# Block 3 of a four-block transformer kernel: the weighted values of a turn in one piece behind the next turn's scores

## The chip, the core and the metric

The kernel runs on one core of a Trainium2 chip. A core has five engines that run side by side, each through its own instructions in its own order: TensorE (PE: matmuls; its weight loads are shown apart as PEld), VectorE (DVE), ScalarE (ACT), GpSimd (POOL) and SyncE (SP), which issues DMAs. They wait for each other through semaphores. Matmul results land in PSUM, which is small (here eight banks of 128 x 512 f32), and another engine copies them to SBUF. The metric is the device time of one execution in microseconds (us); the number given for a kernel is the median of its runs.

## The reference, cut to what matters

Four blocks follow each other on x of shape (2, 1024, 128): an attention with an MLP (two layers), a windowed attention with an MLP (two layers), a local attention with a pooled "latent" part, and a routed mixture of experts. The change is in the third:

```python
def _L1_attn_ref(x, ...):                     # 16 heads of 8, window 128
    qkv = x @ qkv_w + qkv_b
    q, k, v = jnp.split(qkv, 3, axis=-1)
    local = _local_attention(heads(q), heads(k), heads(v))
    pooled = x.reshape(B, nlat, chunk, D).mean(axis=2)
    ...
    remote = lat_out @ rout_w + rout_b
    gate = jax.nn.sigmoid(local @ gl_w + remote_h @ gr_w)
    mixed = gate * local + (1.0 - gate) * remote_h
    return mixed @ out_w + out_b

def _local_attention(q, k, v):
    ...
    scores = jnp.einsum('bhnqd,bhnkd->bhnqk', qb, kb) * scale
    scores = jnp.where(allowed, scores, NEG)
    attn = jax.nn.softmax(scores, axis=-1)
    out = jnp.einsum('bhnqk,bhnkd->bhnqd', attn, vb)
```

Each query sees at most 128 keys before it, so a tile of 128 queries needs the keys of its own tile and of the one before.

## The kernel before, in words

All four blocks stand in one program. In each block the order of the instructions on TensorE, VectorE, ScalarE and GpSimd is written out by hand: they are issued in the order in which the Python code calls them, and each engine runs its own in that order.

Block 3 is the class BlockC (from L1025; stage_c at L1019 runs it). It goes through 16 query tiles (b, m), two sequences of eight, and does each in two **turns** (ip 0 and 1); a turn holds eight heads as two slots of four. Its `both()` issues one turn, as a software pipeline of three turns: the scores of this turn, the transposes of the weights of the turn before (`self.turns`), and the weighted values of the turn before that (`self.values`).

- `score()` (L1241) gives four steps. The first issues on TensorE the masks (L1258, 4 bf16 matmuls that write the mask into PSUM) and the scores (L1262, 32-row matmuls), and on VectorE two row maxima (L1267), one for each of the two score tiles s0 and s1. The second is four exponentials of the first tile on ScalarE (L1271) and, unless a sort is under way, the subtraction for the second tile on VectorE (L1278). The third, in a sort, is four more exponentials (L1271). The fourth, without one, is one wide exponential (L1288).
- `turn()` (L1292), a **group of transposes**: four 128 x 128 transposes of the weights (L1299) into one of two PSUM buffers named tr, and ScalarE's copy of them to pT (L1300). A turn has four such groups.
- `value()` (L1302), a **group of values**: four matmuls whose weights are 32 columns wide (L1310), each in another quarter of the array's columns; in f32 they are 8 loads and 8 passes in the trace. They add up in a bank named o, which `k.mm()` hands out from a pool of two.
- `finish()` (L1316), once a tile: ScalarE copies o to oT (L1319); one beat later or more, `rest()` transposes it (L1326), divides by the sums on VectorE (L1329, L1332) and calls `done()`, which starts `gate()` (L1420) when a group of tiles is complete. From there come the products on GpSimd (L1435), the output matmul (L1472) and the first steps of block 4 (`Front.tiles`, L1541, with L1554, L1560 and the sort of the router's scores, L1524 and L1525).

What else there is to do comes from the pipe (`Pipe`, L109): a list of steps by **beat**. `both()` has four beats; at the head of each, `beat()` issues the steps that are due then, ahead of that beat's own work. `later(0, f)` puts f at the head of the next beat to come. Steps that need a bank of the pool of two take one beat each, in beats 1 to 7 of every eight; the foreign steps that the prediction speaks of (projections L1158 and L1165; the latent part L1358, L1359, L1374, L1380, L1397, L1403; L1326; L1472) stand there. `front.todo` holds the passes of the sort on VectorE; one is issued at the end of each beat.

So in the kernel before a beat of a full turn holds: due steps; one step of this turn's scores; one group of transposes; one group of values; one pass of the sort. The values and finish() of the last turns follow when the scores are through (`while self.turns or self.values or pipe.due`), and behind them block 4 fills TensorE with expert matmuls (L1665) while the sort and the routing run on VectorE.

Of the kernel before, what the change touches and what calls it, by code (L numbers as in the profile page):

```python
# [539 lines left out]
class BlockB:  # L540
# [175 lines left out]
    def project(self, l, b, m, later):  # L716
# [78 lines left out]
        for at, rank, f in (  # L795
            (0, 0, queries), (1, 1, values), (1, 2, square), (6 if first else 2, 1, keep), (2, 2, sums),
            (3, 0, root), (4, 0, scale), (5, 1, cross), (6, 1, straight), (7, 1, both),
        ):
            if not first or f not in early:
                later(at, f, rank=rank)  # L800
# [224 lines left out]
class BlockC:  # L1025
# [61 lines left out]
    def both(self, b=None, m=None, ip=None, nxt=None):  # L1087

        now = self.score(b, m, ip) if m is not None else []
        for i in range(4):  # L1090
            self.pipe.beat()
            for f in now[i : i + 1] + self.turns[i : i + 1] + self.values[i : i + 1]:
                f()
            if nxt and i == 0:
                self.mask(*nxt)
            if not self.hold:
                for f in self.front.todo[:1]:
                    f()
                del self.front.todo[:1]
        for f in self.values[4:]:  # L1100
            self.pipe.later(0, f)
        self.values = self.turns[4:]
        self.turns = []
        if m is not None:
            nk = 1 if m == 0 else 2
            pairs = [(half, t) for half in range(2) for t in range(nk)]
            none = [lambda: None] * (4 - len(pairs))
            self.turns = [lambda p=p: self.turn(b, m, 2 * p[0] + ip, p[1]) for p in pairs] + none
            if nk == 1:
                self.turns = self.turns[:1] + self.turns[2:3] + self.turns[1:2] + self.turns[3:]  # L1110
            self.turns += [lambda p=p: self.value(b, m, 2 * p[0] + ip, p[1]) for p in pairs] + none
            if ip == 1:
                self.turns.append(lambda: self.finish(b, m))
# [703 lines left out]
def route(k, p1, front, fill):  # L1817
# [84 lines left out]
    for step in (8, 4, 2, 1, 0):  # L1902
# [70 lines left out]
    both = junk[:, :P]  # L1973
    nc.vector.scalar_tensor_tensor(
        both, ps[:, :P], 1.0, k.mat["pair"], ALU.mult, ALU.mult, accum_out=v
    )
    nc.vector.tensor_tensor(v, v, none, ALU.add)
# [268 lines left out]
```

## Time and profile before

| | us |
|---|---|
| three runs | 1286.54, 1290.57, 1290.62 |
| median of the runs | 1290.57 |
| span of the profiled execution, first to last instruction | 1288.7 |
| block 1 | about 0 to 366 |
| block 2 | about 366 to 757 |
| block 3 | about 757 to 1046 |
| sort and routing of block 4, with expert matmuls beside them | about 1046 to 1146 |
| rest of block 4 | about 1146 to 1289 |
| first and last masks of block 3 (L1258) | 766.75 and 1027.23 |

The profile is of one execution; the trace holds no other time of it than its span, so sums are made against 1288.7. Over the span TensorE is busy 90%, VectorE 68%, ScalarE 50% and GpSimd 38%.

How its lines read: a group line gives source line, engine, operation, out<-in by the program's names, shapes and count; then busy us and the mean ns of one; then the engine's idle time just ahead of these instructions and what ended it. A row in order of time gives the start (us from the span's start), how long the row lasts, engine, line and what it is; in brackets the idle time ahead of it. Rows of equal instructions are merged (x4, x8). A line of busy time by stretch gives the stretch, its length, then PE, PEld, DVE, ACT and POOL busy us with counts, the clock granted to TensorE (1.00 is full), DMA share and GB/s.

### The profile page before, as it was taken

The numbers are of one execution on the slowest core, as the hardware profiler recorded it, in microseconds if no ns is written. First come the engines' busy times: TensorE is split into PE (matmuls) and PEld (weight loads), VectorE is DVE, ScalarE is ACT, GpSimd is POOL, SyncE is SP. The second block draws the span as 40 slices with busy tenths as digits, with TensorE's granted clock in tenths as the row PEclk, the third lists the DMA queues.
The fourth block names the chain that finished last, engine by engine and source line by source line (L and its number), as shares of the span: only waits on it lengthen the run. The fifth ranks groups of instructions, "written<-read, shape, count | busy, mean of one in ns | idle before, by whom it ended". The sixth has DMA issues, their size and how long they took to land.

```text
span 1288.7 us, 23486 instructions
## 1 busy us (share of the span) xinstructions
PE 1158.7 (90%) x9441; PEld 747.7 (58%) x9441; DVE 870.0 (68%) x1782; ACT 646.3 (50%) x1216; POOL 488.6 (38%) x565
## 2 busy tenths in 40 slices
PE   5999999999688999999999877989999978997798
PEld 3656766666356656666656634546555543433688
DVE  5556666555587776776777435556677979999763
ACT  5445455444355665665664545656665755441000
POOL 1523333232588776676686442221222211100000
PEclk9899999999899999999999988989998989999799
DMA  9000000000010000010100021000000000000000
GB/s 297 2 1 1 1 1 1 2 1 1 18 26 22 22 22 18 22 26 18 26 22 18 5 78 41 1 1 1 2 1 1 2 1 1 0 17 1 25 17 17
DMA packets 19840, 25.18 MB, mean 20 GB/s; under 512 B 2762, under 2 KB 13716, under 8 KB 19476
## 3 DMA queue, kind: packets, MB, share of 16 engines
q1 hardware_dynamic: 19076, 23.02, 6.4%
q8 instruction: 75, 1.23, 0.4%
q10 hardware_dynamic: 656, 0.66, 0.2%
q14 instruction: 33, 0.27, 0.1%
HBM read 13.32 MB, written 1.05 MB: 11 GB/s over the span
## 4 chain that ended last, share of the span: by engine, by line
PE 61%; DVE 23%; ACT 7%; POOL 5%; issue 4%; DMA 0%; DVEq 0%; POOLq 0%; ACTq 0%
PE big L1665 6%; PE mm L1748 5%; PE bank L407 4%; PE s L372 4%; PE bank L960 4%; PE s L727 3%; PE s L835 3%; PE bank L880 2%; PE s L1262 2%; PE s L1258 2%; PE bank L467 2%; PE tr L1299 2%; DVE nm L1267 2%; PE bank L488 2%; DVE nm L378 2%
## 5 line engine op out<-in xcount | busy, mean ns | idle before, releaser
L1267 DVE TENSOR_REDUCE nm<-s 128x4 f32<-128x1024 f32 (+1 forms) x64 | 71.0, 1152 | 60.1 <-PE s L1262 59.8
L378 DVE TENSOR_REDUCE nm<-s 128x1 f32<-128x1024 f32 x64 | 75.1, 1216 | 51.4 <-PE s L372 51.4
L1300 ACT COPY pT<-tr 128x512 f32<-128x512 f32 x120 | 70.0, 598 | 73.2 <-PE tr L1299 73.0
L774 POOL TENSOR_TENSOR t<-raw,tab 128x512 f32<-128x512 f32 x62 | 77.1, 1266 | 75.0 <-DVE raw L765 75.0
L1299 PE MATMUL tr<-ident,pr 128*128 128x128 f32 x480 | 77.2, 284 | 2.6 <-ACT pT L1300 2.3
L736 ACT ACTIVATE sq<-s 128x1024 f32<-128x1024 f32 x32 | 32.7, 1023 | 86.8 <-PE s L727 86.8
L384 ACT ACTIVATE pr<-s,nm 128x1024 f32<-128x1024 f32 x64 | 71.0, 1120 | 8.3 <-DVE nm L378 8.2
L395 PEld LDWEIGHTS bank<-ident,pr 128*128 128x128 f32 x512 | 57.4, 143 | 30.0 <-issue 22.5
L781 POOL TENSOR_TENSOR raw<-raw,tab 128x1024 f32<-128x1024 f32 x31 | 73.1, 2360 | 2.4
L788 POOL TENSOR_TENSOR raw<-raw,t 128x1024 f32<-128x1024 f32 x31 | 73.2, 2363 | 1.7
L407 PE MATMUL bank<-pT,v 128*64 128x128 f32 x1024 | 73.1, 287 | 0.7 <-DVE pT L400 0.2
L1674 ACT ACTIVATE hid<-big,cols 128x512 f32<-128x512 f32 x62 | 41.9, 687 | 60.4 <-PE big L1665 60.4
L1665 PE MATMUL big<-xTd,d_gate 128*128 128x512 f32 x128 | 67.1, 613 | 5.1 <-DVE r_above L1915 2.5
L1665 PE MATMUL big<-xTd,d_up 128*128 128x512 f32 x128 | 68.8, 628 | 2.7 <-DVE r_above L1912 2.0
L407 PEld LDWEIGHTS bank<-pT,v 128*64 128x64 f32 x1024 | 57.8, 142 | 22.6 <-issue 11.5
L398 ACT COPY pT<-bank 128x512 f32<-128x512 f32 x64 | 34.9, 587 | 68.3 <-PE bank L395 68.3
L1299 PEld LDWEIGHTS tr<-ident,pr 128*128 128x128 f32 x480 | 54.7, 144 | 21.0 <-issue 11.6
L395 PE MATMUL bank<-ident,pr 128*128 128x128 f32 x512 | 66.5, 280 | 0.0
L372 PE MATMUL s<-kk,q 64*128 64x512 f32 x256 | 64.7, 615 | 0.6 <-ACT pr L384 0.5
L1748 PEld LDWEIGHTS mm<-d_down,hid 128*128 128x128 f32 x496 | 61.0, 196 | 5.7 <-DVE xo L1779 1.9
L727 PE MATMUL s<-b_wqkv,hT 128*128 128x512 f32 x128 | 62.8, 613 | 1.7 <-ACT hT L694 1.3
L1748 PE MATMUL mm<-d_down,hid 128*128 128x128 f32 x496 | 61.7, 280 | 1.3 <-DVE xo L1779 1.3
(368 smaller groups left out, 2843.4 us busy)
## 6 DMA issues: line engine op xcount, KB each, us to landing
vs<-v SPq DMA_DIRECT2D x60, 130.0 KB, 2.2
b_wqkv<-in_L_ffn_wqkv_dram SPq DMA_DIRECT2D x2, 768.0 KB, 8.9
b_tab<-in_c_xpos_dram SPq DMA_DIRECT2D x1, 1024.0 KB, 8.0
d_up<-in_L_ffn_Wup_dram SPq DMA_DIRECT2D x1, 1024.0 KB, 5.4
d_gate<-in_L_ffn_Wgate_dram SPq DMA_DIRECT2D x1, 1024.0 KB, 7.3
out_dram<-xo SPq DMA_DIRECT2D x3, 256.0 KB, 2.3
rows<-in_rows_dram SPq DMA_DIRECT2D x1, 760.0 KB, 6.7
b_w<-in_L_ffn_w_dram SPq DMA_DIRECT2D x2, 341.0 KB, 7.7
```

The source lines that it names most:

```text
L372: nc.tensor.matmul(t["s"][h][:, keys], q[rows, qt * P : (qt + 1) * P], kk[rows, keys], start=True, stop=True,)
L378: nc.vector.tensor_reduce(t["nm"][h], t["s"][h], AX.X, ALU.max, negate=True)
L395: nc.tensor.transpose(ps[:, i * P : (i + 1) * P], t["pr", h][:, at : at + P], k.ident)
L407: nc.tensor.matmul(t["u"][h * 64 : h * 64 + 64, :P], v[:, kb, h * 64 : h * 64 + 64], t["pT"][:, h, kb], start=(kb == 0), stop=(kb == MT - 1),)
L727: nc.tensor.matmul(qk[:, cut], lhsT, k.b_wqkv[:, l, cut], start=True, stop=True)
L774: nc.gpsimd.tensor_tensor(t2[:, :, :, a : a + 32], r4[:, :, :, z : z + 32], tab(1)[:, :, None, a : a + 32].to_broadcast([P, 2, 8, 32]), AL ...
L781: nc.gpsimd.tensor_tensor(r4, r4, tab(0)[:, :, None, :].to_broadcast([P, 2, 8, 64]), ALU.mult)
L788: eng.tensor_tensor(flat, flat, t["t2"].rearrange("p j h d -> p (j h d)"), ALU.add)
L1267: nc.vector.tensor_reduce(nm[h], view[h], AX.X, ALU.max, negate=True)
L1299: nc.tensor.transpose(ps[:, c * P : (c + 1) * P], pr[:, c, t * P : (t + 1) * P], k.ident)
L1665: self.k.nc.tensor.matmul(ps, weights[:, rows], self.xT[:, cut], start=True, stop=True)
L1748: nc.tensor.matmul(sums[part][:, cols], hid[tp, h, c][:, e, cols], k.d_down[:, c + 8 * e, :], start=start and e == 0, stop=False,)
```

## The change

The values leave the four beats and stand together in the first beat, behind the scores and ahead of the first group of transposes. finish(), the fifth entry of `self.values` in each second turn, was set down at the end of the turn for the head of the next turn's first beat; now it is set down behind the first beat, for the head of the second beat of the same turn.

```diff
@@ both() @@
         now = self.score(b, m, ip) if m is not None else []
         for i in range(4):
             self.pipe.beat()
-            for f in now[i : i + 1] + self.turns[i : i + 1] + self.values[i : i + 1]:
+            for f in now[i : i + 1] + (self.values[:4] if i == 0 else []) + self.turns[i : i + 1]:
                 f()
+            if i == 0:
+                for f in self.values[4:]:
+                    self.pipe.later(0, f)
             if nxt and i == 0:
                 self.mask(*nxt)
             ...
-        for f in self.values[4:]:
-            self.pipe.later(0, f)
         self.values = self.turns[4:]
```

In order on TensorE, with S for masks and scores, T for a group of transposes, V for a group of values and x for foreign steps at the head of a beat: before, `x S T V | x T V | x T V | x T V`; after, `x S V V V V T | x T | x T | x T`. On ScalarE, the first copy (L1300), then in each second turn finish()'s copy (L1319), then the exponentials (L1271); before, L1319 stood ahead of the first copy. Nothing is added or removed; what is computed is the same.

## The prediction

> **What bounds the kernel now.** I read first the page's costliest groups, for who waits for whom in block 3 (L1019 to L1489), then its busy time by stretch, then one turn of it in order of time, row by row.
>
> ```profile
> L1267 DVE TENSOR_REDUCE nm<-s 128x4 f32<-128x1024 f32 (+1 forms) x64 | 71.0, 1152 | 60.1 <-PE s L1262 59.8
> L1300 ACT COPY pT<-tr 128x512 f32<-128x512 f32 x120 | 70.0, 598 | 73.2 <-PE tr L1299 73.0
> L1299 PE MATMUL tr<-ident,pr 128*128 128x128 f32 x480 | 77.2, 284 | 2.6 <-ACT pT L1300 2.3
> ```
>
> VectorE and ScalarE spend 60 and 73 us idle for TensorE, TensorE 2.6 us for the copies: at this height block 3 is TensorE's. The busy times (us, then PE, PEld, DVE, ACT, POOL, granted clock) agree, and show a clock that is not always full:
>
> ```profile
> 757.00:1046.00 289.00, 260.18 (x2514) 158.50 (x2512) 189.97 (x381) 180.34 (x383) 71.95 (x101) 0.94 0.04 14
> ...
> 793.00:854.00 61.00, 54.79 (x569) 34.06 (x569) 36.07 (x67) 41.19 (x85) 7.78 (x12) 1.00 0.00 1
> 854.00:861.00 7.00, 6.45 (x24) 3.02 (x28) 1.79 (x5) 0.35 (x1) 4.53 (x4) 0.51 0.00 0
> ```
>
> TensorE is busy 260 of 289 us. But a busy TensorE is not yet a bound; the order inside a turn tells more. This is the turn from 907.38 us (its masks) to 913.83 (the next turn's masks), with one foreign step (L1403, 0.64 us) in it:
>
> ```profile
> 909.42 0.66 PE L1299 MATMUL tr<-ident,pr 128*128 128x128 f32 x4
> 909.52 2.36 DVE L1267 TENSOR_REDUCE nm<-s 128x4 f32<-128x1024 f32 x2 [3.40 <-PE s L1262]
> 910.00 0.16 PEld L1310 LDWEIGHTS mm<-pT,v 128*32 128x32 f32 x8 [0.17 <-issue]
> ...
> 910.17 0.58 ACT L1300 COPY pT<-tr 128x512 f32<-128x512 f32 x1 [1.70 <-PE tr L1299]
> 910.36 0.52 PEld L1403 LDWEIGHTS mm<-c_rout,latT 32*128 32x128 f32 x4 [0.20 <-issue]
> ...
> 910.78 1.57 ACT L1271 ACTIVATE pr<-s,nm 128x256 f32<-128x256 f32 x4
> ...
> 912.22 1.09 ACT L1300 COPY pT<-tr 128x512 f32<-128x512 f32 x2
> ...
> 912.88 0.42 PEld L1299 LDWEIGHTS tr<-ident,pr 128*128 128x128 f32 x4 [0.20 <-ACT pT L1300]
> ...
> 913.83 0.55 PEld L1258 LDWEIGHTS <-identb 128*128 128x128 bf16 x4 [0.20 <-issue]
> ```
>
> The scores end at 909.42. First transposes T0 go at once; ScalarE copies them out (910.17), then does the first four exponentials (910.78), for which the first row maxima came at 909.52 + 1.18 = 910.70, then the second copy (912.22). There are two `tr` buffers, so the fourth transposes T3 need that second copy: they start at 912.88, released by L1300. Their values and the next scores follow. So here the turn is already set by copy, exponentials, copy on ScalarE, just level with TensorE's own row of work. TensorE waits little because the four groups of values stand in that time.
>
> **The change, part by part.** *Cheaper values.* T to V takes 910.00 - 909.42 = 0.58 us, V to the next step 910.36 - 910.00 = 0.36 (0.16 of loads, 0.20 of gap). Four of each: 3.76 us. The trace has two groups of values standing together once:
>
> ```profile
> 846.41 0.38 PEld L1310 LDWEIGHTS mm<-pT,v 128*32 128x32 f32 x16 [0.17 <-issue]
> ...
> 846.98 0.55 PEld L1258 LDWEIGHTS <-identb 128*128 128x128 bf16 x4 [0.20 <-DVE v L1170]
> ```
>
> Two cost 0.57, so a second group costs 0.21, and four together 0.36 + 3 x 0.21 = 0.99. Transposes behind transposes start 0.47 apart (L1326 at 904.65, L1299 at 905.12), so four take 1.88. New sum 2.87: TensorE's work falls by 0.89 us a turn. Directly behind the scores (32-row loads) a value group does not occur in the trace; transposes there start after a gap of 0.33, into values 0.17 elsewhere: -0.2 to +0.2 a turn (6 us either way over 29 turns, kept for the range); I take 0, as both neighbours pay a gap of this kind already.
>
> [...]
>
> *Later transposes.* The four groups stand in front of T0, on the way to ScalarE. T0 starts 0.99 later, 910.41; its copy at 911.16 (0.75 after T0, as now); the exponentials behind it in ScalarE's order at 911.16 + 0.52 = 911.68 (copies follow each other by about 1.09 - 0.57 = 0.52) instead of 910.78: +0.90. The second copy 1.44 later, 913.12; T3 0.66 after that, 913.78; the next scores 0.47 later, as no values stand behind T3: 914.25 against 913.83, **+0.42**.
>
> *The earlier finish.* finish() now comes at beat 1 of the turn with the values instead of at the head of the next turn. It issues L1319 on ScalarE (914.80 in the trace, 0.59 us, in the time of the scores, where ScalarE has nothing else). Now it stands between the first copy and the exponentials of each second turn, another 0.5: those turns **+0.92**. Queued behind it are the exponentials, for which T3 and the next turn wait. In exchange its bank is free three steps earlier, and rest(), done() and gate() come earlier, with their few GpSimd steps (72 of 289 us busy) and VectorE steps. No moved step issues a DMA; SP's queue is not touched. The fourth group reads the copy that the last turn ended with (914.34 to 914.91), hidden behind the scores, which end at 915.87; without that cover it would cost up to 0.6.
>
> *Over the block.* From the first masks (766.75) to the last (1027.23) are 31 turns in 260.5 us. A turn gains up to 0.89 where TensorE's order alone decides. Five early ones (778 to 827 us) carry the projections (L1158, L1165, about 1 us each): between -0.89 and -0.4, I take 5 x -0.65 = -3.2. Of the 22 turns behind them some 11 show T3 (L1299's loads) released by L1300; these pay in full, half 0.42, half 0.92: 11 x 0.67 = +7.4. In the other 11, foreign steps of 1 to 2.4 us stand before T3 and cover between none and all of it; they end in copies on the same ScalarE queue, so I take half: +3.6. *The tail:* the last values have L1403 and L1472 and their waits between them (1041.98 to 1045.3); placed together they let the last finish start about 2.9 earlier, and the gate, the last sort and the routing hang on it: -2.9. Sum -3.2 + 7.4 + 3.6 - 2.9 = **+4.9 us**.
>
> [...]
>
> *The clock.* Stretches at 0.50 to 0.53 of the clock start at 782, 854, 963 and 990.6 us. Ahead of the one at 854 TensorE idles 2.2 us (L1215 waits for VectorE). What such a stretch costs stands in its rows:
>
> ```profile
> 856.68 1.22 PE L1359 MATMUL mm<-rkd,rqT 32*128 32x256 f32 x2
> 857.83 1.89 PE L1258 MATMUL s<-mask_c,identb 128*128 128x512 bf16 x4
> 859.64 1.75 PE L1262 MATMUL s<-kT,qm 32*128 32x256 f32 x16
> ```
>
> Elsewhere these take 0.69 (twice a stretch), 1.04 and 1.15: 2 x 0.53 + 0.85 + 0.60 = 2.5 us a stretch. The change leaves TensorE 0.89 us less work in a turn that is 0.4 to 0.9 longer, so its 29 us of idle in block 3 about double (22 x 1.5). Between no and four more stretches, 0 to 10; I take one and a half: **+3.8**.
>
> Against the profiled execution: 1288.7 + 4.9 + 3.8 = 1297.4 us of span. The median of the runs is 1.9 above that span, so the forecast is **1299**.
>
> **The rivals.** *TensorE decides (faster).* Place: T3. Price: -0.89 a turn. It decides where foreign steps before T3 exceed what ScalarE needs: T3 comes 0.99 + 3 x 0.47 = 2.4 plus x behind the scores on TensorE, 913.78 - 909.42 = 4.36 (4.9 with finish) on ScalarE, so from x = 2 to 2.5 us. For it: 73 us of ScalarE's idle behind L1299. Against: most turns have x of 0.7 to 1.7. If half of 29 turns were so and the others level: 14 x -0.89 - 2.9 = -15, **1275**. Chance 0.10.
>
> *A draw.* The foreign steps hide the 0.42 and 0.92 in all but the 11 turns, the clock as before: -3.2 + 7.4 - 2.9 = +1.3, **1292**. Against it: several foreign steps (L1326, L1374) wait for ScalarE themselves. Chance 0.18.
>
> *The clock falls in each second pair of turns* (five stretches more, and all 22 turns pay 0.67): -3.2 + 14.7 - 2.9 + 12.5 = +21, **1312**. For it: the doubled idle. Against: the clock falls only behind long single waits now. Chance 0.12.
>
> That the change might not do what it says: the values' only condition is the copy at 914.91, so they can stand where it puts them; I give this nothing.
>
> **How the numbers follow.** My forecast has 0.60: 1295 to 1308 (all 22 turns between 0.3 and 0.67, none to four stretches). The range 1288 to 1311 takes in the draw, leaves out the faster case and most of the third rival. A measurement of this kernel can tell about 0.3% (3.9 us) from no change: slower than 1294.5 is the forecast and the third rival, 0.72; within, 0.18; faster, 0.10.
>
> **What would show it.** Right: in a plain turn L1310's 32 rows stand in one piece of about 1 us; L1299 starts about 1 us behind the scores; T3 waits over 1 us for L1300; L1271 starts 0.9 (with L1319 before it 1.4) later than now; ScalarE's idle behind L1299 does not shrink by the 0.89 a turn; the last finish is nearer to the last scores; more stretches at 0.5. Wrong: turns that get shorter behind 827 us, or T3 that finds its copy done; then TensorE decided. A different size with the same rows means that the clock or the cover by foreign steps was misjudged.

## The result, and the profile after

| | before | after |
|---|---|---|
| median of six runs each (us) | 1288.67 (1284.18 to 1290.62) | 1294.23 (1292.07 to 1296.48) |
| ratio, 95% interval | | 1.0051 [1.0033, 1.0069] |
| span of the profiled execution | 1288.7 | 1291.5 |
| first masks of block 3 (end of what lies ahead) | 766.75 | 765.37 |
| first to last masks ("the block") | 260.5 | 270.1 |
| last masks to the end ("the tail") | 261.5 | 256.1 |

The ratio isn't that of the two medians. The change makes the kernel 0.5% slower. In the two profiled executions, 9.6 us are lost in the block, 5.4 us won in the tail, and 1.4 us less pass in what lies ahead, whose instructions are the same. In the changed kernel all lines of block 3 behind L1093 are one higher (transposes L1300, copy L1301, values L1311, exponentials L1272, finish()'s copy L1320, its transposes L1327).

The costliest groups of the kernel after (busy, mean ns of one, idle time ahead and what ended it):

```profile
L1268 DVE TENSOR_REDUCE nm<-s 128x4 f32<-128x1024 f32 (+1 forms) x64 | 71.1, 1152 | 66.0 <-PE s L1263 66.0
L1301 ACT COPY pT<-tr 128x512 f32<-128x512 f32 x120 | 70.9, 607 | 88.9 <-PE tr L1300 88.7
...
L1300 PE MATMUL tr<-ident,pr 128*128 128x128 f32 x480 | 76.0, 285 | 8.1 <-ACT pT L1301 7.8
```

All three wait longer: VectorE 66.0 us for the scores (59.8 before), ScalarE 88.7 for the transposes (73.0), TensorE's transposes 7.8 for the copies (2.3). Both ends of the hand-over wait more: a chain through both has become longer, while the busy times of the three have hardly changed (71.1, 70.9 and 76.0 us against 71.0, 70.0 and 77.2). The busy times of block 3 (us, then PE, PEld, DVE, ACT, POOL, granted clock), in a window cut like the one before:

```profile
755.60:1053.00 297.40, 246.48 (x2516) 166.78 (x2514) 192.77 (x387) 177.34 (x386) 73.73 (x106) 0.93 0.04 14
```

TensorE is busy 14 us less (246 against 260) in a stretch 8 us longer. The values did get cheaper; the time went into waiting. The turn of the prediction, row by row, now from 906.18 us (its foreign step is now L1327, at 911.10, and no longer L1403, as finish() and with it rest() have moved):

```profile
908.21 1.08 PE L1311 MATMUL mm<-pT,v 128*32 128x128 f32 x32
908.31 2.36 DVE L1268 TENSOR_REDUCE nm<-s 128x4 f32<-128x1024 f32 x2 [3.03 <-PE s L1263]
909.22 0.86 PEld L1300 LDWEIGHTS tr<-ident,pr 128*128 128x128 f32 x8 [0.20 <-issue]
...
909.97 0.58 ACT L1301 COPY pT<-tr 128x512 f32<-128x512 f32 x1 [2.44 <-PE tr L1300]
910.45 0.59 ACT L1320 COPY oT<-mm 128x512 f32<-128x512 f32 x1
...
910.93 1.58 ACT L1272 ACTIVATE pr<-s,nm 128x256 f32<-128x256 f32 x4
...
912.36 1.11 ACT L1301 COPY pT<-tr 128x512 f32<-128x512 f32 x2
...
913.04 0.66 PE L1300 MATMUL tr<-ident,pr 128*128 128x128 f32 x4 [0.85 <-ACT pT L1301]
...
913.53 0.59 PE L1259 MATMUL s<-mask_c,identb 128*128 128x512 bf16 x2
```

The piece stands at 908.21 and T0 at 909.22, 1.01 us behind it. Everything behind T0 moved by that, and from the exponentials on by finish()'s copy as well: measured from the turn's masks, the exponentials start at 4.75 us (3.40 before), T3 at 6.86 (5.50), the next masks at 7.35 (6.46).

### The profile page after: what moved, and what is told of

Its sections match the earlier page's. It is cut to its first block, busy times and chain, and to the rows that moved or that the text cites. A ratio compares the mean times of both kernels' runs of the same rounds, so it can differ in the third digit from the quotient of the medians.

```text
span 1291.5 us, 23484 instructions
## 1 busy us (share of the span) xinstructions
PE 1138.6 (88%) x9441; PEld 751.5 (58%) x9441; DVE 871.2 (67%) x1781; ACT 643.6 (50%) x1219; POOL 487.8 (38%) x565
## 4 chain that ended last, share of the span: by engine, by line
PE 59%; DVE 22%; ACT 10%; POOL 5%; issue 4%; DMA 0%; DVEq 0%; ACTq 0%; POOLq 0%
PE big L1666 6%; PE mm L1749 5%; PE bank L407 4%; PE s L372 4%; PE bank L960 4%; PE s L727 3%; PE s L835 3%; PE bank L880 2%; PE s L1263 2%; ACT pr L1272 2%; PE bank L467 2%; PE bank L488 2%; DVE nm L378 2%; PE s L1259 2%; PE bank L395 2%
## 5 line engine op out<-in xcount | busy, mean ns | idle before, releaser
L1268 DVE TENSOR_REDUCE nm<-s 128x4 f32<-128x1024 f32 (+1 forms) x64 | 71.1, 1152 | 66.0 <-PE s L1263 66.0
L1301 ACT COPY pT<-tr 128x512 f32<-128x512 f32 x120 | 70.9, 607 | 88.9 <-PE tr L1300 88.7
L1300 PE MATMUL tr<-ident,pr 128*128 128x128 f32 x480 | 76.0, 285 | 8.1 <-ACT pT L1301 7.8
L384 ACT ACTIVATE pr<-s,nm 128x1024 f32<-128x1024 f32 x64 | 71.1, 1120 | 7.6 <-DVE nm L378 7.5
L407 PEld LDWEIGHTS bank<-pT,v 128*64 128x64 f32 x1024 | 57.2, 141 | 22.4 <-issue 11.3
L1300 PEld LDWEIGHTS tr<-ident,pr 128*128 128x128 f32 x480 | 54.9, 145 | 22.0 <-ACT pT L1301 11.8
L1272 ACT ACTIVATE pr<-s,nm 128x256 f32<-128x256 f32 (+1 forms) x164 | 63.0, 481 | 0.5 <-DVE nm L1268 0.5
```

Source lines behind the costliest of these rows:

```text
L407: nc.tensor.matmul(t["u"][h * 64 : h * 64 + 64, :P], v[:, kb, h * 64 : h * 64 + 64], t["pT"][:, h, kb], start=(kb == 0), stop=(kb == MT - 1),)
L1272: nc.scalar.activation(prs[h][:, c, :w], view[h][:, c], AF.Exp, bias=nm[h][:, c : c + 1])
L1300: nc.tensor.transpose(ps[:, c * P : (c + 1) * P], pr[:, c, t * P : (t + 1) * P], k.ident)
```

## The experiments

One number serves as a probe below: the length, masks to masks, of this same turn, which has the full clock (1.00) in every kernel ("the plain turn"). In e9, e10 and e11 the trace lacks the first mask matmul of this turn and of the last; there the plain turn is taken from scores to scores, and the last masks from their weight loads. (In the others scores to scores and masks to masks agree to 0.01 us.) The plain turn's foreign step is L1403 where finish() is late and in e6, L1327 in after, e5, e7 and e8. "Half clock" is the time in the block that lies in stretches with a granted clock of 0.50.

| kernel | median | ratio to before, 95% | block | half clock | tail | plain turn |
|---|---|---|---|---|---|---|
| before | 1288.67 | | 260.5 | 30.7 | 261.5 | 6.46 |
| after | 1294.23 | 1.0051 [1.0033, 1.0069] | 270.1 | 35.9 | 256.1 | 7.36 |
| e1 behind T2 | **1275.93** | 0.9910 [0.9892, 0.9928] | 249.2 | 17.1 | 259.6 | 5.98 |
| e2 behind T0 | 1288.32 | 1.0004 [0.9989, 1.0019] | 260.0 | 27.0 | 264.3 | 6.09 |
| e3 after, late finish | 1299.19 | 1.0089 [1.0070, 1.0109] | 267.8 | 37.1 | 264.4 | 6.87 |
| e4 tail only | 1289.28 | 1.0009 [0.9997, 1.0020] | 260.5 | 30.7 | 262.0 | 6.45 |
| e5 behind T0, early finish | 1287.58 | 1.0003 [0.9990, 1.0016] | 266.4 | 33.6 | 255.1 | 6.85 |
| e6 behind T2, earlier finish | 1286.53 | 0.9992 [0.9976, 1.0009] | 261.4 | 42.1 | 259.1 | 5.99 |
| e7 after, finish behind exps | 1300.84 | 1.0109 [1.0085, 1.0133] | 278.9 | 46.1 | 255.4 | 7.80 |
| e8 after, T2 twice | 1289.91 | 1.0026 [1.0010, 1.0041] | 270.2 | 30.5 | 254.5 | 7.36 |
| e9 two and two | 1285.57 | 0.9984 [0.9975, 0.9993] | 256.3 | 20.5 | 262.2 | 6.43 |
| e10 behind T3 | 1287.27 | 0.9991 [0.9978, 1.0004] | 261.1 | 30.7 | 261.0 | 7.10 |
| e11 behind T1 | 1281.95 | 0.9953 [0.9938, 0.9968] | 252.7 | 28.9 | 262.4 | 5.99 |

Medians come from 5 to 12 runs, each ratio from runs of the kernel before on the same chip (1288.0 to 1288.9); block, half clock, tail and plain turn come from the one profiled execution, while the runs of one kernel spread over 1 to 9 us.

Two pairs show what half clock costs. Turns are counted here from scores to scores. From e1 to e6, the 20 turns that have the full clock in both are 1.2 us shorter in sum; the other 11 are 13.4 us longer, with 26.9 us more of half clock. From e1 to e11, 23 such turns are 0.6 us longer in sum; the other 8 are 3.8 us longer, with 13.7 us more of half clock. So a microsecond at half clock costs some 0.3 to 0.5 us, an estimate, as the order in those turns differs too. Where two kernels below differ in half clock, that much of their difference comes from the clock and not directly from the order.

**e1: the piece behind T2, finish() at its old place.** The same four groups in one piece, where TensorE waits anyway.

```diff
-            for f in now[i : i + 1] + self.turns[i : i + 1] + self.values[i : i + 1]:
+            for f in now[i : i + 1] + self.turns[i : i + 1] + (self.values[:4] if i == 2 else []):
```

> The four groups of values in one piece, but behind the third group of transposes instead of behind the scores; finish() as before the change. Theory (the piece costs because it keeps T0, and with it the first copy and the exponentials on ScalarE, 0.99 us back): T0 and the exponentials stand as before, the piece lies in the wait for the second copy, T3 comes when it came (3.46 us behind the scores in a plain turn) and the next scores 0.47 instead of 0.95 behind it: about 0.5 less in a plain turn, up to 0.89 where TensorE decides. Over 29 turns, with part of it lost to foreign steps, 6 to 14 us faster than before. Rival (the piece itself costs, by its place in the array or by the bank it holds, wherever it stands): slower than before by about 5 us, as the changed kernel.

1275.93 us, 13 us below the kernel before. The plain turn (masks at 900.80) in order of time:

```profile
902.83 0.42 PEld L1299 LDWEIGHTS tr<-ident,pr 128*128 128x128 f32 x4 [0.33 <-issue]
...
904.20 1.57 ACT L1271 ACTIVATE pr<-s,nm 128x256 f32<-128x256 f32 x4
905.08 0.81 PEld L1310 LDWEIGHTS mm<-pT,v 128*32 128x32 f32 x32 [0.17 <-issue]
...
905.64 1.09 ACT L1300 COPY pT<-tr 128x512 f32<-128x512 f32 x2
906.29 0.42 PEld L1299 LDWEIGHTS tr<-ident,pr 128*128 128x128 f32 x4 [0.40 <-ACT pT L1300]
```

T0 follows on the scores, the exponentials start 3.40 us behind the masks, as before, and the piece fills the time in which T3 waits for its copy: only 0.40 us of that wait is left. So the making of one piece isn't what costs; its place is. The block is 11.3 us shorter than before, with 13.7 us less of half clock: by the estimate above, 4 to 7 us of it are clock. The 23 turns at full clock in both kernels are 5.0 us shorter in sum.

**e2: the piece behind T0.** The diff of e1 with `i == 0`.

> The piece behind the first group of transposes; finish() as before the change. Theory: the first copy and the exponentials come on time again, so the loss of the changed kernel goes; but the foreign steps of the second beat come 0.6 us later, and where they end in a copy ahead of the exponentials they push these. Between 8 us faster and 2 slower than before, less gain than with the piece behind T2. Rival (only the saved switches count): the same gain as with the piece behind T2, as both save six a turn.

1288.32 us, against e1's 1275.93 with as many switches: changes of the weights' shape in TensorE's order, 128*128 in transposes and 128*32 in values (in the kernel before the loads idle 0.17 us ahead of the values at 910.00 and 0.20 us behind them, at 910.36). T0 is on time, and the loss of the changed kernel is gone, but there is no gain over before. The plain turn is 6.09, nearly that of e1; the block is 10.8 us longer than e1's, with 9.9 us more of half clock (3 to 5 us by the estimate), and the tail 4.7 us longer.

**e3: the changed kernel with finish() put back** to the head of the next turn.

```diff
-            if i == 0:
-                for f in self.values[4:]:
-                    self.pipe.later(0, f)
 ...
+        for f in self.values[4:]:
+            self.pipe.later(0, f)
         self.values = self.turns[4:]
```

> The changed kernel with finish() at the head of the next turn again. Theory: each second turn gets back up to 0.5 us (L1319's copy no longer ahead of the exponentials), of which half is covered: first to last masks about 4 us shorter than the 270.1 of the changed kernel; the tail loses the 2.9 us that the early finish gave: in all 4 to 9 us slower than before. Rival (the copy ahead of the exponentials is the whole loss): within 2 us of before.

1299.19 us, 5 us slower than the changed kernel: the early finish() is a gain on balance. The plain turn is 6.87, and its rows show T0's share of the lateness alone (masks at 907.90):

```profile
909.93 1.08 PE L1310 MATMUL mm<-pT,v 128*32 128x128 f32 x32
...
910.95 0.66 PE L1299 MATMUL tr<-ident,pr 128*128 128x128 f32 x4
...
912.17 1.57 ACT L1271 ACTIVATE pr<-s,nm 128x256 f32<-128x256 f32 x4
...
914.28 0.66 PE L1299 MATMUL tr<-ident,pr 128*128 128x128 f32 x4 [1.02 <-ACT pT L1300]
```

Exponentials at 4.27 (3.40 before), the next masks at 6.87 (6.46). The rest of the changed kernel's 7.36 is finish()'s copy. Over the block e3 is 7.8 us longer than e2, which has T0 on time; 10.1 us more of half clock go with that, 3 to 5 us of it by the estimate.

**e4: the new order in the turns without scores only** (the last few), the old one in the others.

```diff
+            late = self.values[i : i + 1] if m is not None else self.values[:4] if i == 0 else []
-            for f in now[i : i + 1] + self.turns[i : i + 1] + self.values[i : i + 1]:
+            for f in now[i : i + 1] + self.turns[i : i + 1] + late:
                 f()
+            if m is None and i == 0:
+                for f in self.values[4:]:
+                    self.pipe.later(0, f)
```

> The kernel before, with the new order only in the last turns that have no scores (values in one piece, finish() one beat later). Theory: the tail's gain is the earlier finish: last masks to end 3 to 5 us shorter, 3 to 5 us faster than before. Rival (the tail got shorter because the longer turns before it had let the sort get further): within 1.5 us of before.

1289.28 us: no gain. The last finish() starts 2.9 us earlier, but nothing of that is left at the last router scores. finish()'s last copy, and the last router scores, in the kernel before:

```profile
1045.37 0.58 ACT L1319 COPY oT<-mm 128x512 f32<-128x512 f32 x1 [3.63 <-PE mm L1310]
...
1068.45 0.38 ACT L1603 COPY r_sT<-mm 128x256 f32<-128x256 f32 x1 [0.17 <-DVE r_zab L1602]
```

and in e4:

```profile
1042.44 0.58 ACT L1324 COPY oT<-mm 128x512 f32<-128x512 f32 x1 [1.17 <-PE mm L1315]
...
1063.76 1.26 ACT L1679 ACTIVATE hid<-big,cols 128x512 f32<-128x512 f32 x2 [2.52 <-PE big L1670]
...
1069.23 0.37 ACT L1608 COPY r_sT<-mm 128x256 f32<-128x256 f32 x1
```

2.9 us earlier at the copy, 0.8 us later at the scores. Between the two lies a longer stretch of half clock in e4 (10.2 us from 1048.4, against 6.8 us from 1052.1), and the router's exponentials stand behind a ScalarE step (1063.76) that waits 2.52 us for an expert matmul. So what the earlier finish() would give at the same clock isn't shown.

**e5: the changed kernel with T0 ahead of the piece**, finish() still early.

```diff
-            for f in now[i : i + 1] + (self.values[:4] if i == 0 else []) + self.turns[i : i + 1]:
+            for f in now[i : i + 1] + self.turns[i : i + 1] + (self.values[:4] if i == 0 else []):
```

> The changed kernel with one swap: the next turn's first transposes (T0) stand ahead of the piece of four weighted-value groups, and finish() keeps its early place. Theory (the loss comes from T0 and all that follows it standing 1 us later; the shorter tail comes from the early finish()): the block is about as long as that of the kernel with the piece behind T0 and the late finish() (260 us), plus about 2 us for the early finish() (270.1 against 267.8 us between the changed kernel and the one with finish() put back), and the tail 5 to 8 us shorter than its 264 us: 1280 to 1286 us. Rival (the early finish() pays only because the block is long): 1287 to 1291 us.

1287.58 us, 6.6 below the changed kernel by this one swap. It lies above the theory's band and inside the rival's. The tail did get as short as expected (255.1 against e2's 264.3); but the block got 6.5 us longer than e2's, not 2. The early finish() gives the tail, and in the plain turn it costs 0.76 us (6.85 against 6.09): its copy stands ahead of the exponentials and has to wait for the piece itself:

```profile
910.53 0.59 ACT L1320 COPY oT<-mm 128x512 f32<-128x512 f32 x1 [0.40 <-PE mm L1311]
```

But the 19 turns that have the full clock in both kernels are 2.1 us shorter in sum. The block's loss lies in the other turns, with 6.6 us more of half clock; how much of it is the copy isn't shown.

**e6: e1 with finish() one beat earlier**, at the head of the turn's last beat.

```diff
+            if i == 2:
+                for f in self.values[4:]:
+                    self.pipe.later(0, f)
 ...
-        for f in self.values[4:]:
-            self.pipe.later(0, f)
```

> The piece behind T2, as in the fastest run so far (1275.9 us), and finish() one beat earlier, behind the same turn's T3 instead of at the head of the next turn. Theory (an earlier finish() shortens the tail only where the router's scores come a whole turn earlier): 1 to 4 us faster, 1272 to 1275 us. Rival (the output copy of 0.59 us now stands ahead of ScalarE's wide exp, which the next turn's T2 and T3 wait for, in each second turn): 2 to 7 us slower, 1278 to 1283 us.

1286.53 us, 10.6 slower than e1, more than the rival gave. finish() stands ahead of T3 here, not behind it as the expectation has it; on ScalarE its copy stands ahead of the wide exponential either way. The rows that the rival is about:

```profile
910.43 0.64 ACT L1320 COPY oT<-mm 128x512 f32<-128x512 f32 x1
...
910.91 1.11 ACT L1289 ACTIVATE pr<-pr 128x1024 f32<-128x1024 f32 x1
```

The wide exponential starts 0.27 us behind the next turn's masks (910.64); in e1's same turn it starts with them (906.79 and 906.79). But the plain turn is no longer than in e1 (5.99 against 5.98), and the turn behind it only 0.16 us. Nearly the whole loss lies in turns that meet half clock, 42.1 us of it against 17.1: e6 is slower by the clock, and the rival's price is not seen in the sum of the other turns (0.1 us). How the moved finish() leads to that clock isn't shown.

**e7: the changed kernel with finish() one beat later**, so that its copy stands behind the exponentials.

```diff
             if i == 0:
                 for f in self.values[4:]:
-                    self.pipe.later(0, f)
+                    self.pipe.later(1, f)
```

> The changed kernel with finish() one beat later, so that its output copy (0.59 us) stands behind the four narrow exps and not ahead of them; the piece stays behind the scores. Theory of the prediction (the copy ahead of the exps makes 0.5 us in each second turn that the chain sets): 2 to 5 us faster than the changed kernel, 1289 to 1292 us, with a tail like its 256 us. Rival (ScalarE's row is full from T0's copy to the wide exp, so the copy delays the same transposes wherever it stands): 1293 to 1297 us.

1300.84 us: neither. It is 6.6 us slower than the changed kernel, with the same tail (255.4). The plain turn is 7.80, and its rows show where its 0.44 us more come from:

```profile
919.25 0.61 ACT L1301 COPY pT<-tr 128x512 f32<-128x512 f32 x1
919.71 0.64 ACT L1320 COPY oT<-mm 128x512 f32<-128x512 f32 x1
920.19 0.65 ACT L1301 COPY pT<-tr 128x512 f32<-128x512 f32 x1
...
920.40 0.66 PE L1327 MATMUL mm<-ident,oT 128*128 128x128 f32 x4 [1.78 <-ACT oT L1320]
```

The transposes of rest() (L1327) move along with finish(); they now stand ahead of T3 in TensorE's order and wait 1.78 us for the output copy, while the copy that T3 needs was done by 919.86. The step that was moved brought its follower into the queue of the critical one. The block has 10.2 us more of half clock as well, so the 6.6 us are not this wait alone.

**e8: the changed kernel with T2's transposes done twice** into the same tile: work of 0.42 us more in the wait ahead of T3.

```diff
-        for c in range(4):
+        for c in (0, 1, 2, 3) * (2 if slot > 1 and t == 0 and m > 0 else 1):
             nc.tensor.transpose(ps[:, c * P : (c + 1) * P], pr[:, c, t * P : (t + 1) * P], k.ident)
```

> The changed kernel with the third transposes of a turn (T2) done twice into the same tile, 0.42 us of TensorE work more in the wait ahead of T3. Theory that the TensorE clock costs a part of the loss (about 3.8 us in the prediction, from half-clock stretches that follow on the longer waits): fewer of these stretches in the block (9 in the changed kernel) and 1289 to 1293 us. Rival (the stretches cost little; turns that TensorE sets get 0.4 us longer): as many stretches, 1295 to 1301 us.

1289.91 us, in the theory's band, 4.3 below the changed kernel; the two intervals against before overlap, and the profiled spans differ by 2.0. Half clock in the block falls from 35.9 to 30.5 us, from seven stretches (the expectation says nine) to four, and the loads' wait for the copies from

```profile
PEld tr L1300 <- ACT pT L1301: 11.8, 18, 1.5
```

in the changed kernel (us in total, times, longest) to this in e8:

```profile
PEld tr L1300 <- ACT pT L1301: 5.0, 10, 1.1
```

But the block isn't shorter (270.2 against 270.1). So 26 more groups of transposes, 26 x 0.42 = 10.9 us of TensorE, leave the block as long as it was. The plain turn stays at 7.36 to 0.01 us: there TensorE's work is free. It isn't everywhere: the five turns with projections are 1.3 us longer in sum, and turns that meet less half clock win it back. The 2.0 us of the profiled spans lie ahead of the block (0.6) and in the tail (1.6), not in the block. So the theory's band held, but a gain by the clock in the block isn't shown.

**e9: two groups behind the scores, two behind T2.**

```diff
-            for f in now[i : i + 1] + self.turns[i : i + 1] + self.values[i : i + 1]:
+            for f in now[i : i + 1] + (self.values[:2] if i == 0 else []) + self.turns[i : i + 1] \
+                    + (self.values[2:4] if i == 2 else []):
```

> Half the dose: two of the four weighted-value groups stand behind the scores, ahead of T0 (some 0.57 us), the other two behind T2; finish() at its late place. Theory (each us of values ahead of T0 makes everything behind it later by that much, and values behind T2 lie in the wait ahead of T3): the plain turn halfway between 5.98 us (all behind T2) and 6.87 us (all behind the scores), 6.3 to 6.6 us, and the time about halfway between 1275.9 and 1299.2 us: 1283 to 1292 us. Rival (only the last few tenths of lateness count, since the exps wait for VectorE's maxima as well as for T0's copy): 1276 to 1282 us.

1285.57 us, in the theory's band, and outside the rival's; the plain turn is 6.43, halfway between e1's 5.98 and e3's 6.87, as expected. In that turn the loss goes with the dose.

**e10: the piece behind T3.** The diff of e1 with `i == 3`.

> The piece of four groups behind the turn's last transposes (T3), finish() at its late place: nothing is ahead of T0, and nothing fills the wait ahead of T3. Theory (the place pays only where TensorE waits anyway): T3 is as early as before, and the next scores start 1 us instead of 0.47 us behind it, plain turn about 7.0 us against 6.46; 1293 to 1303 us. Rival (any contiguous piece pays, wherever it doesn't delay T0): 1276 to 1288 us.

1287.27 us, no different from before; the theory's time was missed and the rival's band held. The plain turn is 7.10, 0.64 longer than before, close to the 7.0 that the theory gave. Here the theory was right about a turn that the chain sets and wrong in the sum: other turns are shorter. Over the five turns with projections (scores to scores, from 776.62 us before and 775.24 in e10) e10 takes 47.4 us against 51.0 before, with 3.4 us less of half clock, so that 1 to 2 of these 3.6 us are clock by the estimate.

**e11: the piece behind T1.** The diff of e1 with `i == 1`.

> The piece behind the second transposes (T1), finish() at its late place. Theory: T2 starts 1 us later, but its copy on ScalarE stands behind the exps and T1's copy and is not late; T3's wait is filled from the front as with the piece behind T0 or T2. Plain turn 5.9 to 6.2 us, time between those of the two neighbours (1288.3 behind T0, 1275.9 behind T2): 1276 to 1288 us. Rival (T2's copy becomes late and T3 with the wide exp's next use behind it): 1289 us or more.

1281.95 us, between its neighbours as expected, and the plain turn of 5.99 is in the band too. It is as short as e1's (5.98), and yet the kernel is 6 us slower than e1: the block is 3.5 us longer, with 28.9 us of half clock against 17.1, and the tail 2.9 us.

## Why the prediction was right, and where not

*The number: within the range, in its lower third.* Forecast 1299, range 1288 to 1311, measured 1294.23. That is nearer to the draw's 1292, and just under the 1294.5 from which the prediction counted "slower"; that line stood on a median before of 1290.57 from three runs, and six give 1288.67. Against those the change is clearly slower. The span grew by 2.8 us, where 8.7 were predicted.

*What bounds the turn: right.* The working gave T0 3.03 us behind the masks (measured 3.04), the first copy 3.78 (3.79), T3 6.90 with finish()'s copy (6.86), the next scores 0.92 later than before (0.90). Without that copy, in e3, the exponentials came 0.87 later (0.90 predicted) and the next scores 0.41 (0.42). Taking the chain through ScalarE row by row, with the order of each engine, gave every one of these to 0.05 us. One sign fell a little short: T3 waits 0.85 us for the copy in this turn, not over 1.

*Cheaper values: right.* The piece takes 1.01 us (predicted 0.99). Nothing shows of the 0.2 us either way directly behind the scores. Where no copy stands in the way, the piece does pay: the five early turns with projections are 3.0 us shorter in sum, at the same 10.2 us of half clock (3.2 predicted), and e1 shows what one piece is worth in a better place. At the 0.89 us of TensorE's work that the prediction took off a turn, an estimate from the rows of the kernel before, 29 turns would give 26 us if nothing else had to be waited for. The best place measured, e1, has one change between transposes and values more a turn than the changed kernel and gave -13 us, a part of it by the clock.

*The block: right in kind, 2 us too large.* Predicted: -3.2 + 7.4 + 3.6, and 3.8 for the clock, 11.6 in all; measured 9.6. The runs allow to go from before to after in steps: one piece with T0 on time (e2) -0.5 us, T0 behind it (e3) +7.8, the early finish() (after) +2.3. But half clock moves by -3.7, +10.1 and -1.1 us with these steps, so they don't tell the order of the turn from the clock. The half cover of the 11 turns with foreign steps, which was a guess in the middle, can't be checked by itself, as foreign steps changed turns. The sum of the turns behind the five is 12.7 us longer, some 10 to 11 without the clock; 11.0 were predicted.

*The clock: somewhat too large.* There are 7 half-clock stretches in the block in place of 4, and 5.2 us more of half clock; three of the seven are shorter (3.4 us) than any before. At 0.3 to 0.5 us each, the estimate above, that is 1.6 to 2.6 us (3.8 predicted), and 7 to 8 of the 9.6 us are left for the order of the turns. Turn by turn, the 18 that have the full clock in both kernels are 2.2 us longer in sum (the early ones shorter, the plain ones longer), and the 13 that meet half clock in either are 7.4 us longer. The prediction's argument against more stretches, that the clock falls "only behind long single waits", was wrong for the kernel before already. Ahead of its stretch at 990.6 us TensorE is busy 2.83 of 3.41 us, and the one wait of note is this:

```profile
990.68 1.08 PE L1326 MATMUL mm<-ident,oT 128*128 128x128 f32 x4 [0.66 <-DVE prl L1366]
```

*The tail: right in sign by luck, the cause wrong.* Predicted -2.9, because the last values stand together and the last finish() starts earlier. In after the tail is 5.4 us shorter, but the last finish() starts 17.8 us behind the last masks, as late as before (18.1), since the last turns are longer; and e4, which has just that cause, gains nothing as it runs. What shortens the tail is finish() in the turns that have scores. There it runs a turn earlier, and with it the whole way to block 4. The middle one of three copies of router scores in the kernel before:

```profile
1038.69 0.37 ACT L1603 COPY r_sT<-mm 128x256 f32<-128x256 f32 x1 [1.54 <-DVE r_zab L1602]
```

and in the kernel after:

```profile
1029.56 0.37 ACT L1604 COPY r_sT<-mm 128x256 f32<-128x256 f32 x1 [1.27 <-DVE r_zab L1603]
```

Before, it comes 11.5 us behind the last masks; after, 5.9 us ahead of them. So VectorE's sort gets more done while the block still runs: 70 of its 281 instructions (the maxima and minima of L1525 and L1526 in after) start ahead of the last masks in after, e5 and e8, 68 in e7, 64 in e6, and 62 in all kernels with the late finish() (e4 among them, where it is late in the turns that have scores). The tails go with it: 254.5 to 256.1 us, 255.4, 259.1, and 259.6 to 264.4. Counted from the third copy of router scores alone, the rest of the kernel takes 215.8 to 217.2 us in the five with the early finish() and 219.6 to 220.4 in the eight with the late one. So the head start is worth some 3 to 4 us; the rest of the 8.2 us by which after's tail is shorter than e3's lies ahead of that copy; from the last masks to 1180 us the granted clock is 0.94 in e3 and 0.96 in after. The prediction had counted the early finish() as a loss in the block and asked only about the last tile.

*The sum.* Of the 5.9 us by which the span stayed below the 1297.4 predicted, 2.5 are the tail, 2.0 the block, and 1.4 the blocks ahead, where the granted clock from 45.1 to 51.9 us is 0.50 in the kernel before and 1.00 in after.

*The rivals.* TensorE does not decide: e8 adds 10.9 us of work to it, and the block stays at 270.1. The draw's time came close, but its account did not hold: behind the five early turns the block is 12.7 us longer, not 7.4, and half clock grew. The heavy fall of the clock (five stretches more, all turns paying in full) did not come. In the changed kernel the copies do hold TensorE back: T3 waits 0.85 us for one in the plain turn. But that isn't a property of the cheaper values: with the piece behind T2 the same copies leave room for a plain turn 0.48 us shorter than before.

What stays open: why the stretches of half clock lie as they do. e1, e2 and e11 have plain turns within 0.11 us of each other and half clock of 17.1, 27.0 and 28.9 us. That e1 fills T3's wait doesn't explain it alone: in the plain turn T3's loads wait 0.40 us in e1 and only 0.22 in e11. With that it stays open how much of the distance between the kernels would remain at one clock.

## What to carry to other kernels

A piece of work that is cheaper in one go still has to be put somewhere: put it in the wait that ends the turn, and not ahead of the instruction whose result another engine needs first. Here the same four groups made the kernel 0.9% slower behind the scores (e3) and 0.9% faster behind T2 (e1), with finish() at its old place in both. Some 6 to 10 of the 23 us between the two are clock, by the estimate above. When a step moves, follow what it issues later as well: finish()'s follower made e7 worse, and a turn's head start for the sort that hangs on finish() made the tail some 3 to 4 us shorter.

## What the runs showed of the hardware

The granted clock falls behind shorter waits than the prediction allowed for ("only behind long single waits", 2.2 us). Busy times in the kernel after (length, PE, PEld, DVE, ACT, POOL, granted clock), around a stretch at 921.0 us:

```profile
917.50:921.00 3.50, 2.33 (x13) 1.31 (x12) 3.43 (x7) 2.79 (x8) 0.65 (x2) 1.00 0.00 0
921.00:924.40 3.40, 2.89 (x11) 2.15 (x12) 0.93 (x1) 2.67 (x5) 2.93 (x3) 0.50 0.00 0
924.40:927.80 3.40, 3.40 (x58) 2.46 (x57) 1.83 (x2) 0.45 (x2) 0.00 (x0) 1.00 0.00 0
```

Matmuls fill 2.33 of the 3.50 us ahead, the only gap of matmuls and loads together has lasted 1.16 us, and the next 3.4 us are at half clock (the wait goes on to 1.68 us). In the traces of before and after the stretches at half clock last 3.4, 6.8, 10.2, 13.7 or 17.1 us. The longest wait in the 6.8 us ahead of the stretches at 921.0, 955.1 and 979.0 us is 1.16, 1.25 and 1.26 us, and 0.66 ahead of the one at 990.6 in the kernel before. So a single wait of 2.2 us is not needed for half clock here; what sets it off isn't shown.
